# The second image's group-norm statistics in pieces of 512 pixels, and two residual chunks in the keys' room

## The chip, the cores and the metric

The kernel runs on one core of a Trainium2 chip. A core has five engines that run side by side, each through its own list of instructions in order: TensorE (PE, matrix products), VectorE (DVE), ScalarE (ACT), GpSimd (POOL) and SyncE (SP). Here SP only issues DMA transfers; ACT issues some as well, between its own work. The metric is the device time of the program in microseconds (us); a run's number is the median over the executions shown.

## The reference

Two residual layers over two images of 512 channels and 64 x 64 pixels, in float32:

```python
# --- layer 0 (conv_preact) ---
x = x + _L0_conv_ref(_gn(x), ...)      # deformable convolution, groups of 32 channels
# --- layer 1 (conv_preact) ---
x = x + _L1_conv_ref(_gn(x), ...)      # attention over the 4096 pixels, batch norm, relu
...
def _gn(v, G=32, eps=1e-5):
    B_, C_, H_, W_ = v.shape
    g = v.reshape(B_, G, C_ // G, H_, W_)
    m = jnp.mean(g, axis=(2, 3, 4), keepdims=True)
    s = jnp.var(g, axis=(2, 3, 4), keepdims=True)
    return ((g - m) / jnp.sqrt(s + eps)).reshape(v.shape)
```

Layer 0 normalizes its input by groups of 16 channels, projects it (`in_w`), and from a depthwise 3 x 3 convolution, a layer norm and a GELU it makes offsets and masks, with which the projection is sampled; `out_w` and the residual follow. Layer 1 normalizes again, makes keys, queries and values, applies softmax attention, and then a batch norm over both images, relu and the residual. The last residual is layer 0's result, so it is read once more at the very end.

## The kernel before

**Layer 0** works in 16 chunks of 512 pixels, eight per image. Each chunk passes through four stages, written as Python generators: `project` (normalize on ACT into `xn`, project on PE, store to `xt` in DRAM), `features` (the nine taps of the convolution: tap 1 on ACT at L790, eight on VectorE at L795 for each of four channel blocks; then the layer norm with two PE sums `p_mean`, L808, and the GELU, L832), `weights` (offsets and masks: PE `po`, L849, VectorE L854 to L897, then `at`, `awT` by PE transposes and ACT copies, L900 and L909) and `sample` (PE `pb` and ACT copies into `bt`, L942; PE `pa`, L956, with ACT copies into `dT`, L967; PE `py`, L976; the residual on VectorE, L981; result stored as `wx`). From L1135 on the order is written out by hand: `period` (L1005) calls single steps of these generators of different chunks, and each engine's list has the order in which these calls are made. In the names of `period`, `f` is a step of `features` of chunk i+2, `w` of `weights` of i+1, `m` of `sample` of i, `y` and `v` the ends of `sample` and `weights` of the chunks before, `p` of `project` of i+3 and `more` a step of the statistics. A period takes about 70 us.

**The statistics** of the input are made by `image_stats` (L704): `bn_stats` on VectorE over pieces, one `bn_aggr` for each channel block, then `group_norm_steps` (L604), a chain between PE, VectorE and ACT. Image 0 is in SBUF as a whole at the start. For image 1 pieces of 256 pixels are loaded by SP into three rotating buffers `xraw`, three ahead, and each call of `more` runs one `bn_stats` and issues the load of a later piece. There are 64 pieces; a period calls `more` 13 times, five periods long. Before the sixth period `run(later)` finishes what is left: the aggregate and the group norm's chain. SP also issues, in its order, `raw` (input rows for `project`, L744), `patch` (what is sampled, L921, eight transfers a time), `res`, `xt` and `wx`.

The key and query weights `wkq` are used only in layer 1 (L1356). They have a buffer of their own and are loaded by SP before the first period (L1131).

**Layer 1** is a loop over the images, and for each over eight query chunks `qb` (L1380). For each, 16 pairs of key blocks `kp` and two further steps accumulate in six PSUM banks (`acc`, L1417); `produce` (L1257) makes scores from `kq` (the keys of an image, 16 KB a partition) two steps ahead. A last product `p7` (L1455) follows; three of its operands `v7` are loaded only while it runs. After the last chunk the residual of image 1 is needed: once `acc` is done, the pools `w1in` (which holds `kq`), `w1v` and `w1vv` are closed (L1441), a pool `rp` of eight buffers of 1 MB is laid over their room, and ACT issues eight loads (L1445). Then come the batch norm's constants (L1518 to L1525) and the final loop: relu on ACT (L1530), the residual's sum on VectorE (L1534), the store by SP (L1535), first image 1, then image 0, whose chunks and residuals are fetched by SP (L1512) into buffers that become free.

Every transfer issued by SP or ACT takes one of eight semaphores in turn, over both engines, and its issuer waits until the transfer eight earlier has landed; this comes from the layer that builds the program.

Of the kernel before, what the change touches and what calls it, by code (L numbers as in the profile page):

```python
# [9 lines left out]
F32 = mybir.dt.float32  # L10
# [7 lines left out]
P = 128  # L18
NB = 2
C = 512  # L20
KB = C // P
H = W = 64
S = H * W
# [7 lines left out]
CH = 512  # L31
NCH = S // CH
# [5 lines left out]
DQ = 64  # L38
# [532 lines left out]
def window_path(ctx: ExitStack, tc: tile.TileContext, t_in: dict, out: bass.AP, far: bass.AP, sums: bass.AP):  # L571
# [26 lines left out]
    norm0 = []  # L598


    wkq = const.tile([P, KB, 3, DQ], F32, name="wkq")
    al = const.tile([P, 1], F32, name="al2")

    def group_norm_steps(mv, k, small, psum, result):  # L604
# [30 lines left out]
    with ExitStack() as l0:  # L635
# [68 lines left out]
        def image_stats(n):  # L704

            mv = sm.tile([P, KB, 2], F32, name="gn_mv")
            size = CH if n == 0 else CH // 2
            pieces, ahead = deque((kb, h) for kb in range(KB) for h in range(S // size)), deque()
            for kb in range(KB):
                st = sm.tile([P, 16, 6], F32, name="gn_st")  # L710
                for h in range(S // size):
                    if n == 0:
                        t = img[kb][:, h * size : (h + 1) * size]
                    else:
                        while len(ahead) < 3 and pieces:
                            k2, h2 = pieces.popleft()
                            ahead.append(io.tile([P, size], F32, name="xraw", bufs=3))
                            nc.sync.dma_start(ahead[-1], x_v[n, :, k2, h2 * size : (h2 + 1) * size])
                        t = ahead.popleft()
                    nc.vector.bn_stats(st[:, h, :], t)  # L720
                    yield
                nc.vector.bn_aggr(mv[:, kb, :], st[:, : S // size].rearrange("p a b -> p (a b)"))
            yield
            result = []
            yield from group_norm_steps(mv, KB, sm, ps, result)
            sc, bi = result
            gn[n] = [sm.tile([P, KB], F32, name=f"gn_{k}{n}") for k in ("scale", "bias")]
            nc.vector.tensor_copy(gn[n][0], sc)
            nc.vector.tensor_copy(gn[n][1], bi)
# [275 lines left out]
        def period(y, v, m, w, f, g, p, more):  # L1005

            p()  # L1010
            y()
            v(4)
            f(4)
            y()
            for taps in (9, 7, 6, 6):
                m(2)
                w()
                more()
                f(taps)
                w()  # L1020
                more()
            w()
            m()
            w()
            m()
            f()
            y()
            f()
            m()
            p()  # L1030
            w(2)
            y(2)
            w()
            m()
            p()
            f()
            w(2)
            p()
            y(2)
            f()  # L1040
            y()
            m()
            p()
            more()
            for k, steps in enumerate((1, 2, 2, 2)):
                p()
                w(steps)
                if k == 0:
                    f()
                p()  # L1050
                more()
                if k < 3:
                    m()
                if k == 0:
                    f()
                if k == 2:
                    g()
            w()
# [68 lines left out]
        run(features(1), project(2), output_bias())  # L1127
        fetch(0, 0)
        fetch(0, 1)
        for k, name in enumerate(("wkT", "wqT", "wkT")):  # L1130
            nc.sync.dma_start(wkq[:, :, k, :], t_in[name].rearrange("(kb p) m -> p kb m", p=P))  # L1131
        for h in range(2):
            nc.sync.dma_start(al[h * DQ : (h + 1) * DQ, :], t_in["L1_conv_align_w"])
        later, y, f = image_stats(1), Chain(sample, NSEQ), Chain(features, 2)
        with tc.manual_schedule():  # L1135
            f()
            for i in range(NSEQ):
                if i == NCH - 3:
                    run(later)
                w, m, g = Chain(weights, i + 1), Chain(sample, i), Chain(features, i + 3)  # L1140
                if i + 2 >= NSEQ:
                    (next_to_last if i + 1 < NSEQ else last_period)(y, v, m, w)
                    y, v = m, w
                    continue
                period(y, v, m, w, f, g, Chain(project, i + 3), lambda: next(later, None))
                y, v, f = m, w, g
            y.rest()
# [5 lines left out]
    with ExitStack() as l1, tc.manual_schedule():  # L1153
# [8 lines left out]
        with ExitStack() as at, ExitStack() as inner:  # L1162
            aw = at.enter_context(tc.tile_pool(name="w1w", bufs=1))
            wk = at.enter_context(tc.tile_pool(name="w1work", bufs=2))
            iw = inner.enter_context(tc.tile_pool(name="w1in", bufs=1, side="right", reuse_waits="tile"))
            vw = inner.enter_context(tc.tile_pool(name="w1v", bufs=3, side="right"))
            vv = inner.enter_context(tc.tile_pool(name="w1vv", bufs=3, side="right"))
            ps = at.enter_context(tc.tile_pool(name="w1ps", bufs=1, space=PSUM))
# [170 lines left out]
            for n in range(NB):  # L1339
# [40 lines left out]
                for qb in range(NCH):  # L1380
                    acc = {}
                    for kp in range(NPAIR + 2):
                        if kp + 2 < NPAIR:
                            produce(qb, kp + 2)
                        if kp == NPAIR - 1:

                            pr = ps.tile([P, 2, CH], F32, tag="st", name="pr")[:, 0, :]
                            nc.tensor.matmul(pr, ones, tots.pop(qb), start=True, stop=True)
                            nc.vector.tensor_mul(xq, xq, pr.unsqueeze(1).to_broadcast([P, KB, CH]))
                            x4 = xq.rearrange("p (h r) (j q) -> p h r j q", h=2, j=2)  # L1390
                            tx = wk.tile([P, 2, 4, HQ], F32, tag="tx", name="tx", bufs=1)
                            nc.vector.tensor_sub(tx[:, :, 3, :], x4[:, 1, :, 1, :], x4[:, 0, :, 1, :])
                            nc.vector.tensor_add(tx[:, :, 0, :], tx[:, :, 3, :], x4[:, 0, :, 0, :])
                            nc.vector.tensor_sub(tx[:, :, 2, :], tx[:, :, 0, :], x4[:, 1, :, 0, :])
                            nc.vector.tensor_sub(tx[:, :, 1, :], x4[:, 0, :, 1, :], x4[:, 0, :, 0, :])
                            rin = wk.tile([P, CH], F32, name="rin", bufs=1)
                            nc.vector.reciprocal(rin, pr)
                        nxt = qb * NPAIR + min(kp, NPAIR) + 2
                        if kp < NPAIR and nxt < NCH * NPAIR:
                            ready.append(load_values(n, nxt % NPAIR))  # L1400
                        if kp == 2:
                            xq = wk.tile([P, KB, CH], F32, tag="x", name="xq", bufs=1)
                            nc.sync.dma_start(xq, x1_d[n][qb])
                        if 3 <= kp < NPAIR:
                            v7s[kp - 3] = load_seventh(n, kp - 3)
                        if kp < NPAIR:
                            v = ready.pop(0)
                            e, tt, _ = made[qb, kp]
                            ops = operands(lambda k: e[:, k, :], tt)
                        else:  # L1410
                            v = w7[:, kp - NPAIR]
                            ops = operands(lambda k: x4[:, k // 2, kp - NPAIR, k % 2, :], tx[:, kp - NPAIR])
                        for j in (3, 4, 5, 2, 1, 0) if kp == 0 else (0, 1, 4, 2, 3, 5) if kp == NPAIR else range(6):
                            if kp == 0:
                                acc[j] = bank(j, f"acc{j}")
                            for cb in range(2):
                                nc.tensor.matmul(  # L1417
                                    acc[j][:, cb * HQ : (cb + 1) * HQ], v[:, j, cb * P : (cb + 1) * P], ops[j],
                                    start=(kp + cb == 0), stop=(kp + cb == NPAIR + 2),
                                )  # L1420
                        next(rest, None)
                        if kp == 6:
                            normalize(xq, sc, bi)
                        if kp == 8 and qb + 1 < NCH:
                            queries(qb + 1)
# [13 lines left out]
                    if n + 1 == NB and qb + 1 == NCH:  # L1439

                        inner.close()  # L1441
                        rp = l1.enter_context(tc.tile_pool(name="w1res", bufs=NCH, side="right", reuse_waits="tile"))
                        for ch in range(NCH):
                            res.append(rp.tile([P, KB, CH], F32, tag="xr", name="xr"))
                            nc.scalar.dma_start(res[ch], x1_d[n][ch])  # L1445

# [139 lines left out]
```

## Time and profile before

| | us |
|---|---|
| median of 3 runs (lowest, highest) | 3688.65 (3687.94, 3691.09) |
| the profiled execution | 3685.08 |
| its span, first to last instruction | 3683.3 |
| PE busy | 3410.6 (93%) |
| VectorE busy | 2344.1 (64%) |
| ACT busy | 1307.4 (35%) |
| `conv` on VectorE (L795), 512 instructions | 399.7 |
| `bn_stats` of image 1, 256 pixels, 64 instructions | 25.8, with 8.3 of waits for their loads |
| `bn_stats` of 512 pixels, one | 0.68 |
| `acc` on PE (L1417), 6144 instructions | 1516.5 |

The profile is of one execution. A line of a group gives the line of the program, engine and operation, the tiles, how often, the busy time, the mean of one, and the engine's idle time ahead of these instructions with what ended most of it. A line of a timeline gives start and length in us, then the same, with the idle time ahead in brackets. A line of the table of stretches gives from:to and length, then for each engine its busy time and how many instructions it started, the granted clock of TensorE (1.00 is full), the busy share of the DMA engines and GB/s. Layer 0 ends at about 1255 us.

### The profile page before, as it was taken

What the parts mean: (1) busy time and instruction counts of PE and PEld (TensorE: products, weight loads), DVE (VectorE), ACT (ScalarE), POOL (GpSimd) and SP (SyncE); (2) the same over time, 40 slices, a digit from 0 to 9 for tenths busy, and PEclk for the clock granted to TensorE, in tenths of its full rate; (3) what the DMA queues carried; (4) which work ended last, traced back from release to release, by engine and by line L of the source; (5) the groups of instructions that cost most, each with busy time, mean ns of one, the idle gap of its engine ahead of it and who ended that gap; (6) DMA issues with size and microseconds to landing.
All of it is one profiled execution on the core that took longest, in us unless ns stands there. A gap on an engine that the chain in (4) does not pass through costs nothing.

```text
span 3683.3 us, 39025 instructions
## 1 busy us (share of the span) xinstructions
PE 3410.6 (93%) x15155; PEld 2430.9 (66%) x15155; DVE 2344.1 (64%) x3581; ACT 1307.4 (35%) x1694; POOL 291.5 (8%) x190
## 2 busy tenths in 40 slices
PE   4589998999998999999999999999999999999990
PEld 1355555555555677777777777787777777777770
DVE  5798989999998575554554554467455455545544
ACT  2476777787886421111111111121111111111114
POOL 2112111211211020000000000021000000000000
PEclk9789999999999999999999999999999999999995
DMA  7233442342331444334334433434333343343349
GB/s 245 63 99 112 134 142 83 112 136 85 119 118 66 159 166 174 124 113 160 123 108 145 137 127 115 153 146 187 130 127 116 114 139 112 104 147 122 112 159 395
DMA packets 179653, 499.93 MB, mean 136 GB/s; under 512 B 22112, under 2 KB 63840, under 8 KB 169984
## 3 DMA queue, kind: packets, MB, share of 16 engines
q1 hardware_dynamic: 175680, 471.11, 38.0%
q10 hardware_dynamic: 3744, 26.22, 1.9%
q8 instruction: 121, 1.98, 0.2%
q14 instruction: 76, 0.62, 0.0%
q0 software_dynamic: 32, 0.00, 0.0%
HBM read 405.96 MB, written 91.29 MB: 135 GB/s over the span
## 4 chain that ended last, share of the span: by engine, by line
PE 76%; DVE 14%; DMA 4%; ACT 2%; SPq 1%; issue 1%; POOL 1%; ACTq 0%; DVEq 0%; POOLq 0%
PE acc L1417 42%; DVE conv L795 8%; PE pS L1262 7%; PE p L1455 7%; PE py L976 5%; PE pa L956 4%; PE pv L1302 4%; PE pq L765 4%; PE pk L1356 1%; PE p_mean L808 1%; DMA patch<-xt 1%; DMA out<-ct 1%; DVE o L854 1%; DMA in_w<-in_L_conv_in_w 1%; DVE rstd L827 1%
## 5 line engine op out<-in xcount | busy, mean ns | idle before, releaser
L1417 PE MATMUL acc<-e,v 128*128 128x256 f32 x3072 | 768.3, 386 | 0.0
L1266 ACT ACTIVATE e<-pS 128x1024 f32<-128x1024 f32 x256 | 262.4, 1025 | 1385.9 <-PE pS L1262 1317.5
L1417 PE MATMUL acc<-tt,v 128*128 128x256 f32 x3072 | 748.2, 380 | 0.3
L1417 PEld LDWEIGHTS acc<-e,v 128*128 128x128 f32 x3072 | 566.5, 190 | 233.2 <-issue 165.4
L1417 PEld LDWEIGHTS acc<-tt,v 128*128 128x128 f32 x3072 | 582.4, 190 | 91.0 <-issue 10.6
L1269 DVE TENSOR_TENSOR t<-e 128x256 f32<-128x256 f32 x256 | 108.9, 425 | 761.2 <-ACT e L1266 761.2
L795 DVE SCALAR_TENSOR_TENSOR conv<-xn,L_conv_dw_w_sb,conv 128x504 f32<-128x504 f32 (+1 forms) x512 | 399.7, 795 | 48.4 <-ACT conv L790 36.4
L1279 DVE TENSOR_TENSOR tot<-tot,e 128x512 f32<-128x512 f32 x480 | 330.1, 688 | 8.3
L956 PEld LDWEIGHTS pa<-bt,patch 96*128 96x128 f32 x2048 | 253.0, 198 | 62.8 <-issue 35.1
L1262 PE MATMUL pS<-q,kq 64*128 64x512 f32 x1024 | 289.0, 641 | 0.0
L956 PE MATMUL pa<-bt,patch 96*128 96x128 f32 x2048 | 256.9, 283 | 12.5 <-ACT dT L967 5.8
L942 ACT COPY bt<-pb 96x1024 f32<-96x1024 f32 x124 | 234.7, 2006 | 56.5 <-PE pb L937 56.5
L765 PE MATMUL pq<-in_w,xn 128*128 128x512 f32 x512 | 235.8, 604 | 4.1 <-ACT xn L755 4.1
L976 PE MATMUL py<-dT,L_conv_out_w_sb 128*128 128x512 f32 x512 | 239.0, 612 | 0.0
L1455 PE MATMUL p<-t,v 128*128 128x256 f32 x1024 | 231.6, 382 | 1.9 <-DMA v<-wv 1.9
L1455 PEld LDWEIGHTS p<-t,v 128*128 128x128 f32 x1024 | 192.1, 190 | 48.8 <-issue 21.2
L967 ACT COPY dT<-pa 32x256 f32<-32x256 f32 x496 | 179.9, 363 | 73.5 <-PE pa L956 64.8
L849 PE MATMUL po<-om_w_pg,feat 128*128 128x432 f32 x512 | 200.9, 537 | 0.0
L976 PEld LDWEIGHTS py<-dT,L_conv_out_w_sb 128*128 128x128 f32 x512 | 99.5, 198 | 121.8 <-issue 117.3
L765 PEld LDWEIGHTS pq<-in_w,xn 128*128 128x128 f32 x512 | 93.9, 194 | 108.8 <-issue 93.2
L849 PEld LDWEIGHTS po<-om_w_pg,feat 128*128 128x128 f32 x512 | 92.7, 189 | 89.4 <-issue 88.1
L1262 PEld LDWEIGHTS pS<-q,kq 64*128 64x128 f32 x1024 | 77.1, 184 | 84.9 <-issue 84.9
(204 smaller groups left out, 3721.5 us busy)
## 6 DMA issues: line engine op xcount, KB each, us to landing
v<-wv SPq DMA_DIRECT2D x252, 768.0 KB
patch<-xt SPq DMA_DIRECT2D x256, 192.0 KB
v<-wv SPq DMA_DIRECT2D x256, 128.0 KB
wv<-v SPq DMA_DIRECT2D x32, 896.0 KB
xt<-xj SPq DMA_DIRECT2D x128, 128.0 KB
res<-in_x SPq DMA_DIRECT2D x64, 256.0 KB
wx<-res SPq DMA_DIRECT2D x64, 256.0 KB
xq<-wx SPq DMA_DIRECT2D x16, 1024.0 KB
```

The source lines that it names most:

```text
L765: nc.tensor.matmul(pq, xn[:, kb, 1 + 2 * t : 3 + 2 * t, :].rearrange("p r c -> p (r c)"), in_w[:, kb, :], start=(kb == 0), stop=(kb == KB ...
L795: nc.vector.scalar_tensor_tensor(dst, src, wt, dst, ALU.mult, ALU.add)
L849: nc.tensor.matmul(po[:, : 3 * GP], f[:, kb, t * P : (t + 1) * P], om_w[:, kb].rearrange("p a k g -> p (a k g)"), start=(kb == 0), stop=(k ...
L942: copy(bt[:SN].rearrange("s g q d -> s d (g q)")[:, d0 : d0 + 4, :], pb[:SN])
L956: nc.tensor.matmul(pa[:, p], xp[:SN, p, cb * P : (cb + 1) * P], bt[:SN, 4 * cb : 4 * cb + 4, PX * s + p, :], start=True, stop=True,)
L967: copy(dst, src)
L976: nc.tensor.matmul(py, out_w[:, kb, cb * P : (cb + 1) * P], dT[:, kb, :], start=(kb == 0), stop=(kb == KB - 1))
L1262: nc.tensor.matmul(pS[:, h, :], kq[r, 2 * (kp // 4) + h, c0 : c0 + P], qs[qb][r, :], start=True, stop=True)
L1266: nc.scalar.activation(e.rearrange("p a q -> p (a q)"), pS.rearrange("p h q -> p (h q)"), AF.Exp)
L1279: nc.vector.tensor_add(tots[qb], tots[qb], e2[:, h, :])
L1417: nc.tensor.matmul(acc[j][:, cb * HQ : (cb + 1) * HQ], v[:, j, cb * P : (cb + 1) * P], ops[j], start=(kp + cb == 0), stop=(kp + cb == NPAI ...
L1455: nc.tensor.matmul(p7[:, cb * HQ : (cb + 1) * HQ], v7[:, cb * P : (cb + 1) * P], t3, start=(k + cb == 0), stop=(k + cb == NPAIR + 2),)
```

## The change

There are two parts.

1. The statistics of image 1 use 32 pieces of 512 pixels, loaded by ACT's queue. Two of the three buffers are the halves of a new tile `early` (4 KB a partition); the third is one `xraw`. `wkq` becomes a view of `early`, so its loads move behind the last `bn_stats`, after `run(later)`. A period calls `more` six times, at other places: ahead of the first four taps, behind these, behind the first and the second `weights` piece among the taps, once ahead of the layer norm's `rstd`, and once in the last loop. 30 pieces fall to five periods, and `run(later)` does the last two as well.
2. The pool `w1in` stays open to the end. Two of the eight residual chunks of image 1 go into `kq`'s room, with loads that ACT issues at the step after the last scores were made (`kp` = 14 of the last chunk); `rp` has six buffers and is loaded as before.

```diff
--- before.py
+++ after.py
@@ -598,7 +598,9 @@
     norm0 = []
 
 
-    wkq = const.tile([P, KB, 3, DQ], F32, name="wkq")
+
+    early = const.tile([P, 2, CH], F32, name="early")
+    wkq = early.rearrange("p a q -> p (a q)")[:, : KB * 3 * DQ].rearrange("p (kb k d) -> p kb k d", kb=KB, k=3)
     al = const.tile([P, 1], F32, name="al2")
 
     def group_norm_steps(mv, k, small, psum, result):
@@ -704,22 +706,23 @@
         def image_stats(n):
 
             mv = sm.tile([P, KB, 2], F32, name="gn_mv")
-            size = CH if n == 0 else CH // 2
-            pieces, ahead = deque((kb, h) for kb in range(KB) for h in range(S // size)), deque()
+            room = [early[:, 0], early[:, 1], io.tile([P, CH], F32, name="xraw")] if n else []
+            pieces, ahead = deque((kb, h) for kb in range(KB) for h in range(NCH)), deque()
             for kb in range(KB):
-                st = sm.tile([P, 16, 6], F32, name="gn_st")
-                for h in range(S // size):
+                st = sm.tile([P, NCH, 6], F32, name="gn_st")
+                for h in range(NCH):
                     if n == 0:
-                        t = img[kb][:, h * size : (h + 1) * size]
+                        t = img[kb][:, h * CH : (h + 1) * CH]
                     else:
+
                         while len(ahead) < 3 and pieces:
                             k2, h2 = pieces.popleft()
-                            ahead.append(io.tile([P, size], F32, name="xraw", bufs=3))
-                            nc.sync.dma_start(ahead[-1], x_v[n, :, k2, h2 * size : (h2 + 1) * size])
+                            ahead.append(room[len(pieces) % 3])
+                            nc.scalar.dma_start(ahead[-1], x_v[n, :, k2, h2 * CH : (h2 + 1) * CH])
                         t = ahead.popleft()
                     nc.vector.bn_stats(st[:, h, :], t)
                     yield
-                nc.vector.bn_aggr(mv[:, kb, :], st[:, : S // size].rearrange("p a b -> p (a b)"))
+                nc.vector.bn_aggr(mv[:, kb, :], st.rearrange("p a b -> p (a b)"))
             yield
             result = []
             yield from group_norm_steps(mv, KB, sm, ps, result)
@@ -1010,15 +1013,17 @@
             p()
             y()
             v(4)
+            more()
             f(4)
+            more()
             y()
             for taps in (9, 7, 6, 6):
                 m(2)
                 w()
-                more()
                 f(taps)
                 w()
-                more()
+                if taps in (7, 9):
+                    more()
             w()
             m()
             w()
@@ -1037,18 +1042,19 @@
             w(2)
             p()
             y(2)
+            more()
             f()
             y()
             m()
             p()
-            more()
             for k, steps in enumerate((1, 2, 2, 2)):
                 p()
                 w(steps)
                 if k == 0:
                     f()
                 p()
-                more()
+                if k == 2:
+                    more()
                 if k < 3:
                     m()
                 if k == 0:
@@ -1127,16 +1133,16 @@
         run(features(1), project(2), output_bias())
         fetch(0, 0)
         fetch(0, 1)
-        for k, name in enumerate(("wkT", "wqT", "wkT")):
-            nc.sync.dma_start(wkq[:, :, k, :], t_in[name].rearrange("(kb p) m -> p kb m", p=P))
-        for h in range(2):
-            nc.sync.dma_start(al[h * DQ : (h + 1) * DQ, :], t_in["L1_conv_align_w"])
         later, y, f = image_stats(1), Chain(sample, NSEQ), Chain(features, 2)
         with tc.manual_schedule():
             f()
             for i in range(NSEQ):
                 if i == NCH - 3:
                     run(later)
+                    for k, name in enumerate(("wkT", "wqT", "wkT")):
+                        nc.sync.dma_start(wkq[:, :, k, :], t_in[name].rearrange("(kb p) m -> p kb m", p=P))
+                    for h in range(2):
+                        nc.sync.dma_start(al[h * DQ : (h + 1) * DQ, :], t_in["L1_conv_align_w"])
                 w, m, g = Chain(weights, i + 1), Chain(sample, i), Chain(features, i + 3)
                 if i + 2 >= NSEQ:
                     (next_to_last if i + 1 < NSEQ else last_period)(y, v, m, w)
@@ -1162,7 +1168,7 @@
         with ExitStack() as at, ExitStack() as inner:
             aw = at.enter_context(tc.tile_pool(name="w1w", bufs=1))
             wk = at.enter_context(tc.tile_pool(name="w1work", bufs=2))
-            iw = inner.enter_context(tc.tile_pool(name="w1in", bufs=1, side="right", reuse_waits="tile"))
+            iw = l1.enter_context(tc.tile_pool(name="w1in", bufs=1, side="right", reuse_waits="tile"))
             vw = inner.enter_context(tc.tile_pool(name="w1v", bufs=3, side="right"))
             vv = inner.enter_context(tc.tile_pool(name="w1vv", bufs=3, side="right"))
             ps = at.enter_context(tc.tile_pool(name="w1ps", bufs=1, space=PSUM))
@@ -1419,6 +1425,11 @@
                                     start=(kp + cb == 0), stop=(kp + cb == NPAIR + 2),
                                 )
                         next(rest, None)
+                        if n + 1 == NB and qb + 1 == NCH and kp + 2 == NPAIR:
+
+                            for ch in range(2):
+                                res.append(kq[:, KB * ch : KB * (ch + 1), :])
+                                nc.scalar.dma_start(res[ch], x1_d[n][ch])
                         if kp == 6:
                             normalize(xq, sc, bi)
                         if kp == 8 and qb + 1 < NCH:
@@ -1439,8 +1450,8 @@
                     if n + 1 == NB and qb + 1 == NCH:
 
                         inner.close()
-                        rp = l1.enter_context(tc.tile_pool(name="w1res", bufs=NCH, side="right", reuse_waits="tile"))
-                        for ch in range(NCH):
+                        rp = l1.enter_context(tc.tile_pool(name="w1res", bufs=NCH - 2, side="right", reuse_waits="tile"))
+                        for ch in range(2, NCH):
                             res.append(rp.tile([P, KB, CH], F32, tag="xr", name="xr"))
                             nc.scalar.dma_start(res[ch], x1_d[n][ch])
```

## The prediction

> **What bounds the kernel now.** I read the page's chain of waits first: which engine holds the end, stage by stage.
>
> ```profile
> PE acc L1417 42%; DVE conv L795 8%; PE pS L1262 7%; PE p L1455 7%; PE py L976 5%; PE pa L956 4%; PE pv L1302 4%; PE pq L765 4%; PE pk L1356 1%; PE p_mean L808 1%; DMA patch<-xt 1%; DMA out<-ct 1%; DVE o L854 1%; DMA in_w<-in_L_conv_in_w 1%; DVE rstd L827 1%
> ```
>
> Layer 1 (from about 1255 us) is TensorE's, and the change touches it only at its very end. In layer 0 VectorE (conv L795) and TensorE share the path. So I next cut layer 0 at the starts of `my` (L884), which comes once a period, and read the busy-time table of these stretches:
>
> ```profile
> core 0: us, PE busy (x) PEld busy (x) DVE busy (x) ACT busy (x) POOL busy (x), PEclk, DMA share, GB/s
> 283.13:359.72 76.59, 67.54 (x312) 39.48 (x311) 67.24 (x86) 54.32 (x74) 12.99 (x10) 0.93 0.41 122
> 359.72:433.97 74.25, 66.79 (x308) 39.14 (x307) 66.53 (x85) 53.35 (x72) 12.98 (x10) 0.95 0.40 126
> 433.97:508.22 74.25, 67.20 (x312) 39.44 (x311) 67.05 (x87) 55.02 (x76) 12.97 (x10) 0.98 0.39 125
> 508.22:583.49 75.27, 66.46 (x310) 39.26 (x309) 65.27 (x85) 53.68 (x71) 12.97 (x11) 0.93 0.34 104
> 583.49:654.20 70.71, 67.47 (x318) 39.75 (x317) 62.68 (x72) 55.80 (x77) 12.98 (x11) 1.00 0.35 108
> 654.20:721.91 67.71, 64.50 (x310) 38.31 (x309) 62.68 (x73) 53.86 (x73) 13.00 (x10) 1.00 0.37 113
> ```
>
> A plain period takes 67.7 us at full clock. Those with statistics of the second image take 74 to 77, at a lower clock; the one before these (210.31 to 283.13) takes 72.8. Over six periods the excess is 444 - 6 x 67.7 = 38 us. The timelines of PE and VectorE say what it is made of:
>
> ```profile
> 273.86 2.07 PE L808 MATMUL p_mean<-tot,ones_c 128*128 128x512 f32 x2 [5.75 <-POOL tot L803]
> 275.73 5.75 PE L976 MATMUL py<-dT,L_conv_out_w_sb 128*128 128x512 f32 x8
> ...
> 712.63 1.12 PE L808 MATMUL p_mean<-tot,ones_c 128*128 128x512 f32 x2 [1.23 <-POOL tot L803]
> 713.59 3.60 PE L976 MATMUL py<-dT,L_conv_out_w_sb 128*128 128x512 f32 x8
> ```
>
> ```profile
> 242.90 0.69 DVE L982 BATCH_NORM_STATS2 stats<-res 128x6 f32<-128x512 f32 x1
> 243.51 0.41 DVE L720 BATCH_NORM_STATS2 gn_st<-xraw 128x6 f32<-128x256 f32 x1
> 243.84 6.85 DVE L795 SCALAR_TENSOR_TENSOR conv<-xn,L_conv_dw_w_sb,conv 128x504 f32<-128x504 f32 x9
> ...
> 253.02 0.43 DVE L720 BATCH_NORM_STATS2 gn_st<-xraw 128x6 f32<-128x256 f32 x1 [1.48 <-DMA xraw<-in_x]
> ```
>
> The period's cycle is: VectorE's taps, then POOL's `tot`, then p_mean on PE, then PE's py/pa/pq without a gap, then ScalarE's conv (L790), then the next taps. Whatever stands between the first and the last tap delays p_mean. With statistics there PE idles 5 to 7 us before p_mean instead of 1.23, and the next ten matmuls run slow: 2.07 + 5.75 us against 1.12 + 3.60, 3.1 us more. A step from one start to the next is 0.33 us for 256 pixels and 0.61 for 512.
>
> The end, by the same table: DMA stands still, then is full to the last.
>
> ```profile
> 3560.00:3570.00 10.00, 10.00 (x46) 8.42 (x45) 6.38 (x6) 0.00 (x0) 0.00 (x0) 1.00 0.00 0
> 3570.00:3575.00 5.00, 5.00 (x25) 4.40 (x24) 1.85 (x1) 0.26 (x1) 0.00 (x0) 1.00 0.00 0
> 3580.00:3585.00 5.00, 5.00 (x25) 4.41 (x24) 2.07 (x1) 0.00 (x0) 0.00 (x0) 1.00 1.01 424
> 3640.00:3650.00 10.00, 0.00 (x0) 0.00 (x0) 4.99 (x3) 6.52 (x10) 0.00 (x0) 0.50 1.02 414
> ```
>
> **What the Trainium skill says.** "TensorE: Matmul & The Clock Gate", Part 1: PE falls to half clock after a window of about 3.4 us without enough work, and the windows run free. The trace agrees: gaps of 4.35 to 7.1 us before p_mean were followed by half clock, eight gaps of 1.2 us (periods from 645 us on) were not; a gap of 2.5 us (1294.4) wasn't, one of 1.76 (1230.6) was. "DMA: Bandwidth & Descriptors", Issuing engines are not separate DMA queues: transfers from SP and ACT share the same DMA engines, so ACT's queue adds no bandwidth. Its section Queues, rings and completion order: the engines take turns between the queues, so a load issued by ACT needn't wait behind all that SP has queued. The trace of before has no such load in layer 0, so there it can't be checked.
>
> **The change, part by part.**
>
> *Statistics on the path.* Before, a period has 13 pieces of 256; seven lie between first and last tap: 7 x 0.335 = 2.35 us, and one waits 1.5 to 2.7 us there for its load, which SP issued behind eight patches. After, six pieces of 512. One stands before the first tap and one before `res` (L981), where VectorE waits in a plain period anyway (1.82 us for ScalarE's conv, 1.42 for py): nothing. Two stand among the taps: 1.22 us. Two lie in the TensorE half. With the first they fill the 1.82 us (3 x 0.61), and one of them puts ScalarE's gelu back 0.6 us, of which its 0.73 us gap, less a DMA issue in it, hides most: I add 0.25. So a period is 67.7 + 1.22 + 0.25 = 69.2 us, if the clock holds.
>
> *Load issues on ACT.* 32 of some 0.37 us (as the 64 from SP took). Where they are put ScalarE waits in the plain period: 1.21, 0.38 and 1.15 us around the bt copies, 0.83 and 0.73 around dT. Hidden; uncovered they would be 6 x 0.37 = 2.2 us a period. Each load also waits for its room's bn_stats (one call back, long done) and, as the program shares eight DMA semaphores in turn among SP and ACT, for the transfer eight earlier to land: the fourth and the sixth patch, xt, raw. By the timeline the patches are issued in 0.7 us steps from the first tap on; the sixth should land by 9 us, when ACT comes there. Behind ACT stand the bt copies, and pa and p_mean behind these, with 2.4 us to spare.
>
> *The start.* Before, SP loaded the first pieces at 139.8 us. After, ACT issues them behind the awT copies, which end at 175.7, while VectorE has its first bn_stats ahead of the first tap (170.73). With 2.4 us to land, as a load in the next period took (issued 233.41, used 235.86), plus 0.3 us for the double size, the taps begin at 179.0. After the lighter pieces of that period `my` comes at 217.4 instead of 210.3: 7.1 us lost, once.
>
> *Group norm and key weights.* Two pieces and the aggregate now stand before the group norm's chain: 1.2 us, in the 4.7 us that VectorE waits there for ScalarE's `gn_var`. The five key-weight loads leave SP's queue at 78 us and come back behind these bn_stats, ahead of the raw loads, which have some 40 us: nothing for either; before 170 us I bound it by -1 and +1 us.
>
> *Sum of layer 0:* 217.4 + 4 x 69.2 + (75.27 - 1.4) = 568.1 for the sixth `my`, against 583.5: -15.4 us. (The 1.4 is the rstd wait in that period, due to the cold clock before it.) The clock is what isn't known: PE's gap before p_mean becomes 1.23 + 1.22 = 2.4 us. Bounds: no half clock (0), or about 2.2 us in each of four periods (+9). I take +4: **-11.4 us.**
>
> *The end.* Two of eight residual chunks (2.1 MB) move to the stretch at 3553 us, behind the last exp, where DMA is soon idle. They leave a queue that is full at 415 GB/s: 2.1 / 0.415 = 5.05 us. p7 then waits less for its v7 loads (2.7 us), so the first output is ready 2.6 us earlier. Small gaps in the stream cost 1 to 2 us, since ScalarE gives a chunk each 2.8 us and DMA needs 2.5. Bounds -5.5 and -2.5, **taken -4 us.**
>
> Total -15.4: 3685.1 (the profiled execution: its span 3683.3 and 1.8 around it) gives 3669.7. The median shown is 3.55 above that execution, so 3673.2.
>
> **The rivals.**
> 1. *The clock stays cold.* 2.4 us of gap are still enough in each period: -15.4 + 9 - 4 = -10.4, 3678. For it: the gap of 1.76 us that was followed by half clock. Against: the one of 2.5 that wasn't.
> 2. *The pieces wait for their own loads.* From 398 to 404 us DMA moves 300 to 404 GB/s (three raw loads). If two pieces a period wait 1.8 us each over four periods, 14.4 us come back: -1, 3687, no change.
> 3. *ScalarE is held at the queue (the slower side).* If the patch, xt or raw transfer that an ACT load waits for lands late, ACT stands still ahead of the bt copies and all of layer 0 behind it. Up to 2.4 us a period is hidden; at 8 us in each of five periods it is 5 x 5.6 = 28 us, the total +13: 3701. It decides from 2.4 + 15.4/5 = 5.5 us a period. Against: patches were landing by about 11.6 us after the first tap at the latest.
>
> That the change doesn't do what it says can be left out: 32 pieces, 30 in the periods' calls and two in the closing run, stand in the program.
>
> **How the numbers follow.** Forecast 52% (3666 to 3682 by its bounds), rival 1 20%, rival 2 15%, rival 3 13%. This kernel's measurement tells 0.2% (7.4 us) from no change: the forecast and rival 1 lie below 3681, so faster 72%, same 15%, slower 13%. The range reaches from 3665 (no cold clock, end at its best: -15.4 - 5.5, and 3 more) to 3688, which leaves out rival 3.
>
> **What would show it.** Right: `my` near 217 in the first period, then periods near 69 us; p_mean's gap 2 to 3 us; no wait of bn_stats for DMA but the first, 8 us or more after the last work; L942 waiting for PE alone; 200 GB/s or more between 3553 and 3562. Wrong: bn_stats rows with waits for DMA in each period, idle ScalarE ahead of L942 ended by a DMA, a clock below 1.00 in each period, or an unchanged distance from the last acc matmul to the end.

## The result, and the profile after

The changed kernel takes 3677.86 us (median of 10 runs, 3675.72 to 3680.51), the kernel before beside it 3687.7 (10 runs, 3683.93 to 3691.09): ratio 0.9975, 95% interval 0.9965 to 0.9985. That is 9.8 us faster, where the forecast said 15.4.

I read the profile after in the same order as the one before. First the table of stretches, cut at the starts of `my` (now L887), for the six periods from the first on and a plain one:

```profile
218.37:288.90 70.53, 61.63 (x280) 37.16 (x281) 64.75 (x74) 54.26 (x74) 14.61 (x11) 0.93 0.39 120
288.90:359.92 71.02, 66.28 (x309) 38.78 (x308) 66.33 (x79) 53.57 (x73) 13.05 (x10) 0.98 0.41 130
359.92:431.18 71.26, 66.19 (x310) 38.93 (x309) 66.68 (x80) 53.84 (x73) 13.03 (x10) 0.98 0.40 129
431.18:502.05 70.87, 66.42 (x314) 38.98 (x313) 66.70 (x80) 54.86 (x74) 13.04 (x10) 1.00 0.40 129
502.05:575.90 73.85, 65.07 (x307) 38.61 (x306) 66.36 (x85) 52.88 (x70) 13.03 (x11) 0.93 0.37 115
575.90:646.63 70.73, 67.46 (x317) 39.77 (x317) 62.73 (x73) 55.77 (x77) 13.03 (x11) 1.00 0.34 108
646.63:714.36 67.73, 64.50 (x310) 38.32 (x309) 62.75 (x73) 53.83 (x73) 13.08 (x10) 1.00 0.38 113
```

The first `my` stands at 218.37 (forecast 217.4). The four statistics periods take 70.5 to 71.3 us where before they took 72.8 to 76.6; the forecast was 69.2, plus 1 for the clock. The group norm's period takes 73.85 (forecast 73.87). The sixth `my` is 7.6 us ahead of before, or 9.1 when both are counted from their chunk 0's `my`, which came 1.5 us later in this execution (forecast 11.4).

The start, in the timelines of VectorE and ScalarE:

```profile
173.03 0.16 DVE L1127 TENSOR_TENSOR L_conv_out_b_sb<-L_conv_out_b_sb,p_bias 128x4 f32<-128x4 f32 x1 [8.71 <-PE p_bias L1123]
179.06 0.69 DVE L723 BATCH_NORM_STATS2 gn_st<-early 128x6 f32<-128x512 f32 x1 [5.87 <-DMA early<-in_x]
```

```profile
175.24 1.07 ACT L912 COPY awT<-p_tr 128x512 f32<-128x512 f32 x2
176.08 0.34 ACTq L721 DMA_DIRECT2D early<-in_x  x1
```

The first piece comes at 179.06 and, one step of 0.61 later, the taps at 179.67. The forecast had the taps at 179.0. The load took 3.0 us from issue (176.08) to use; 2.7 was forecast.

Next, TensorE's timeline around `p_mean` in the third and fourth period:

```profile
421.87 1.38 PE L811 MATMUL p_mean<-tot,ones_c 128*128 128x512 f32 x2 [3.10 <-POOL tot L806]
423.04 5.08 PE L979 MATMUL py<-dT,L_conv_out_w_sb 128*128 128x512 f32 x8
...
492.74 1.12 PE L811 MATMUL p_mean<-tot,ones_c 128*128 128x512 f32 x2 [2.50 <-POOL tot L806]
493.70 3.60 PE L979 MATMUL py<-dT,L_conv_out_w_sb 128*128 128x512 f32 x8
```

The gap is 2.5 to 3.1 us, near the forecast's 2.4, instead of 5 to 7. Behind the gap of 3.10 the next matmuls are slow, behind the one of 2.50 they aren't. And VectorE among the taps of the third period:

```profile
400.90 0.60 DVE L857 TENSOR_TENSOR o<-po,om_b_pg 128x432 f32<-128x432 f32 x1
402.07 0.69 DVE L723 BATCH_NORM_STATS2 gn_st<-xraw 128x6 f32<-128x512 f32 x1 [0.57 <-DMA xraw<-in_x]
402.68 1.51 DVE L798 SCALAR_TENSOR_TENSOR conv<-xn,L_conv_dw_w_sb,conv 128x504 f32<-128x504 f32 x2
```

One piece still waits for its load in the second, third and fourth period: 0.50, 0.57 and 0.17 us. Its load was issued at 395.82, 6.2 us before it was read.

The end, in the table of stretches:

```profile
3550.00:3555.00 5.00, 5.00 (x25) 4.40 (x24) 2.52 (x6) 0.00 (x0) 0.00 (x0) 1.00 1.00 386
3555.00:3560.00 5.00, 5.00 (x23) 4.03 (x22) 0.08 (x1) 0.00 (x0) 0.00 (x0) 1.00 0.48 202
...
3575.00:3600.00 25.00, 16.78 (x77) 13.78 (x76) 11.27 (x24) 3.40 (x5) 0.50 (x2) 0.87 1.02 420
3600.00:3605.00 5.00, 0.00 (x0) 0.00 (x0) 2.82 (x4) 5.00 (x8) 0.00 (x0) 0.50 0.80 329
3605.00:3610.00 5.00, 0.00 (x0) 0.00 (x0) 4.18 (x2) 5.00 (x8) 0.00 (x0) 0.50 0.85 327
3610.00:3615.00 5.00, 0.00 (x0) 0.00 (x0) 3.94 (x3) 5.00 (x8) 0.00 (x0) 0.50 0.99 331
3615.00:3620.00 5.00, 0.00 (x0) 0.00 (x0) 3.95 (x3) 5.00 (x9) 0.00 (x0) 0.50 1.03 356
3620.00:3640.00 20.00, 0.00 (x0) 0.00 (x0) 16.31 (x8) 19.10 (x28) 0.00 (x0) 0.50 1.02 417
```

The kernel before, at the same place behind its first output:

```profile
3605.00:3610.00 5.00, 0.00 (x0) 0.00 (x0) 2.56 (x4) 5.00 (x8) 0.00 (x0) 0.50 1.02 421
3610.00:3615.00 5.00, 0.00 (x0) 0.00 (x0) 4.47 (x2) 5.00 (x8) 0.00 (x0) 0.50 1.00 400
```

The two chunks do move in the idle stretch (386 GB/s from 3550 on). But from 3600 to 3620 us the transfers now run at 327 to 356 GB/s, where before they kept to 400 or more. At 415 that is (86 + 88 + 84 + 59) GB/s x 5 us = 1.6 MB not moved, 3.8 us of the 5.05 us that had left the queue. By the column of the busy share the DMA engines stood idle for about half of this, (0.20 + 0.15 + 0.01) x 5 us = 1.8 us; for the other 2 us they were busy, at a lower rate.

The stretches of every profiled execution (us), from the starts of `my` and the last `acc`. "Start" is from chunk 0's `my` to the first period's, "periods" from there to the sixth, "middle" from the last of the sixteen `my` to the end of `acc`, "end" from there to the end of the span:

| kernel | median (before beside it) | start | periods | middle | end |
|---|---|---|---|---|---|
| before | | 84.2 | 373.2 | 2400.2 | 104.3 |
| changed | 3677.86 (3687.7) | 90.7 | 357.5 | 2404.1 | 102.7 |
| part1_only | 3678.77 (3687.42) | 90.8 | 357.2 | 2402.6 | 103.9 |
| part2_only | 3684.08 (3687.42) | 83.7 | 374.2 | 2398.9 | 103.1 |
| primed | 3670.51 (3687.42) | 83.7 | 362.4 | 2400.6 | 102.8 |
| off_taps | 3716.26 (3687.42) | 91.6 | 398.9 | 2400.6 | 102.9 |
| off5 | 3660.42 (3689.35) | 84.4 | 345.4 | 2402.0 | 102.7 |
| warm | 3672.67 (3689.35) | 90.8 | 354.9 | 2401.7 | 102.3 |
| fin4 | 3674.71 (3689.35) | 90.7 | 357.7 | 2403.7 | 101.2 |
| sp_loads | 3677.10 (3689.35) | 84.0 | 368.5 | 2400.7 | 102.8 |
| act_queue | 3693.45 (3687.69) | 89.5 | 373.6 | 2402.4 | 104.3 |
| best | 3657.69 (3687.69) | 84.0 | 345.5 | 2405.1 | 100.6 |

The changed kernel's own row against before: start +6.5, periods -15.7, end -1.5, together -10.7. The middle scatters from 2398.9 to 2405.1 over these executions, though its query chunks take 129.75 us each, in both the kernel before and the changed one. The two differ there by 3.9 us, so two profiled executions can't be subtracted as wholes; the medians (-9.8) come close to the sum of the other three stretches.

### The profile page after: what moved, and what is told of

Same layout as the page of the kernel before. It is cut to its first block, busy times and chain, and to the rows that moved or that the text cites. A ratio compares the mean times of both kernels' runs of the same rounds, so it can differ in the third digit from the quotient of the medians.

```text
span 3678.2 us, 38948 instructions
## 1 busy us (share of the span) xinstructions
PE 3412.8 (93%) x15155; PEld 2432.7 (66%) x15155; DVE 2351.4 (64%) x3549; ACT 1306.7 (36%) x1694; POOL 292.7 (8%) x190
## 4 chain that ended last, share of the span: by engine, by line
PE 78%; DVE 13%; DMA 4%; ACT 2%; issue 1%; POOL 1%; SPq 1%; ACTq 0%; DVEq 0%; POOLq 0%
PE acc L1423 42%; DVE conv L798 9%; PE pS L1268 7%; PE p L1466 6%; PE py L979 5%; PE pq L768 5%; PE pa L959 5%; PE pv L1308 3%; PE pk L1362 1%; PE p_mean L811 1%; DVE o L857 1%; DMA v<-wv 1%; DMA in_w<-in_L_conv_in_w 1%; DMA xraw<-in_x 0%; DMA r<-wc 0%
```

## The experiments

**Each part alone.** part1_only takes the second part out of the changed kernel, part2_only puts it alone into the kernel before.

```diff
 (part1_only)
-            iw = l1.enter_context(tc.tile_pool(name="w1in", ...
+            iw = inner.enter_context(tc.tile_pool(name="w1in", ...
-                        if n + 1 == NB and qb + 1 == NCH and kp + 2 == NPAIR:
-                            for ch in range(2):
-...
-                        for ch in range(2, NCH):
+                        for ch in range(NCH):
```

> The changed kernel without its second part: all eight residual chunks are loaded after the last acc again. Theory (part 1 is worth what the starts of my show, -7.5 us, and part 2 only what the last stretch shows, -1.5): 3680 us, my as in the changed kernel (first period's at 218.4, the sixth at 576, 7.5 ahead of before), last acc to the end of the span 104.3 us as before. Rival (part 2 is worth the 4 us that the prediction gave it, and part 1 the rest): 3682, sixth my at 578 or later. If the half-clock stretches fall where chance puts them in an execution, the single periods may differ from the changed kernel's by 1.7 us each.

> The kernel before with the second part alone: two residual chunks in the keys' room. Theory (the moved loads leave a hole in the transfers before the first output, and only the end of p7 moves, by 1 us): 3686, last acc to the end of the span 102.8, less than 400 GB/s for some 15 us after p7. Rival (prediction's -4: the queue gets shorter by 5 us and stays full): 3683.7, last acc to end 100.3.

part1_only: ratio 0.9977 (0.997 to 0.9984), 3678.77 us. part2_only: 0.9994 (0.9985 to 1.0003). Part 1 is nearly the whole gain; in time alone part 2 can't be told from nothing. The trace shows more: from the last `acc` to the end it is 103.9 to 104.3 in the three kernels without part 2, and 102.3 to 103.1 in the seven that have it and no other change at the end, 1.4 us in the mean. That excludes the prediction's 4 us.

**The first loads early.** In `primed` the first three pieces are loaded by SP ahead of the first period.

```diff
+            if n:
+                for _ in range(3):
+                    load_piece(nc.sync)
+                yield
...
         later, y, f = image_stats(1), Chain(sample, NSEQ), Chain(features, 2)
+        next(later)
```

> The changed kernel with its first three pieces loaded by SP ahead of the first period instead of by ACT behind the awT copies. Theory (the 7 us at the start are the wait for the first load, nothing else): no wait of the first bn_stats, first tap near 172.5, first my at 211.5 instead of 218.4, the whole 3671. Rival (what is gained at the start is lost again in the first periods, since taps there wait for something else or the clock falls once more): first my no earlier than 216, 3676 or more.

Ratio 0.9953 (0.9937 to 0.997), 3670.51 us, 7.3 less than the changed kernel. The start is 83.7 us again. VectorE's timeline has no wait for a load there:

```profile
170.44 1.52 DVE L805 SCALAR_TENSOR_TENSOR conv<-xn,L_conv_dw_w_sb,conv 128x504 f32<-128x504 f32 x2
171.88 0.69 DVE L730 BATCH_NORM_STATS2 gn_st<-early 128x6 f32<-128x512 f32 x1
```

The first `my` came at 207.56, earlier than expected, since this execution's chunk 0 was also some 4 us ahead; the stretch is the measure. The periods gave back 4.8 us: their waits for `xraw` were 1.21, 0.60 and 0.71, and the group norm's period took 76.4. So the start's loss is shown, and that the loads in the periods are tight as well.

**No piece among the taps, first attempt.** `off_taps` puts the two pieces from among the taps ahead of the first tap and ahead of `res`.

```diff
             v(4)
             more()
+            more()
             f(4)
             more()
+            more()
             y()
...
-                if taps in (7, 9):
-                    more()
```

> The changed kernel with the two pieces among the taps moved: two now stand ahead of the first tap and two ahead of res. Theory (a period's excess is the two pieces among the taps, 1.5 us, and the half clock that the longer gap before p_mean brings, 1.7): gap before p_mean 1.3 us, clock 1.00, second to fourth period 68.0 to 68.4 us instead of 70.5 to 71.3, the whole 3666. Rival (loads: a piece close behind another has 4 us at most to land, in the stretch where patches are loaded): bn_stats waits 1 to 2 us for DMA twice a period, periods 70 or more, 3675 to 3679.

The rival, and far worse than its numbers: ratio 1.0079 (1.0063 to 1.0096), 3716.26 us. ScalarE's and VectorE's timelines show why:

```profile
412.19 0.33 ACTq L721 DMA_DIRECT2D xraw<-in_x  x1
412.28 0.62 ACT L912 COPY awT<-p_tr 128x512 f32<-128x512 f32 x1
413.90 1.68 ACTq L721 DMA_DIRECT2D early<-in_x  x2
419.18 0.34 ACTq L721 DMA_DIRECT2D xraw<-in_x  x1
419.55 3.68 ACT L945 COPY bt<-pb 96x1024 f32<-96x1024 f32 x2 [6.65 <-DMA raw<-in_x]
```

```profile
418.45 0.69 DVE L723 BATCH_NORM_STATS2 gn_st<-xraw 128x6 f32<-128x512 f32 x1 [10.77 <-DMA xraw<-in_x]
419.80 0.69 DVE L723 BATCH_NORM_STATS2 gn_st<-early 128x6 f32<-128x512 f32 x1 [0.66 <-DMA early<-in_x]
```

A load is issued where `more` is called, and in ScalarE's list that place lies behind `at` and the `awT` copies, at 412. VectorE is at its place at 407.7 and waits 10.8 us; the load takes 6.3. ScalarE's load at 419.18 waits for that very piece, as its room must be read first, and behind it stand the `bt` copies, idle for 6.65 us (the releaser that the line names, `raw`, is only the last that landed). The loads before it were held as well. The chain of waits, in order of time, shows by what:

```profile
407.07 6.76 DMA patch<-xt
413.83 0.03 ACTq L721
413.86 0.04 issue
413.90 5.88 DMA early<-in_x
```

The load at 413.90 had to wait until a patch had landed. So this is the prediction's third rival at work: ScalarE is held at its queue, first by the transfers that it named (the trace has a second such wait, to 415.15; up to there 2.3 of the 6.65 us have passed), and then, for longer, by a room that had not been read, which the prediction called "long done".

**No piece among the taps, with the loads in time.** `off5` separates the load from the piece. Six pieces are done ahead of the first period; a period has five.

```diff
+        for _ in range(3):
+            load_piece(nc.sync)
         with tc.manual_schedule():
+            for _ in range(6):
+                next(later)
+                load_piece(nc.sync)
...
             more()
+            more()
             f(4)
             more()
             y()
...
-                if taps in (7, 9):
-                    more()
+                if k < 3:
+                    load_piece()
...
+                if k == 1:
+                    load_piece()
                 if k == 2:
                     more()
+                    load_piece()
```

> The changed kernel with no piece among the taps, in a way that gives each load time: six pieces are done ahead of the first period, with loads by SP; a period has five (two ahead of the first tap, one ahead of res, the two in the TensorE half as before), and each load is issued by ACT where its room has long been read and at least 5 us ahead of its use. Theory (a period's excess is the pieces among the taps, their waits for loads, and the half clock that follows): gap before p_mean 1.2 to 1.3 us, clock 1.00 in the second to fourth period, these 67.9 to 68.4 us, first my near 206, sixth near 553, the whole 3655. Rival (loads are late wherever they are issued beside the patches, as in off_taps): bn_stats waits 2 us or more for DMA in each period, periods of 70 us or more, 3665 or more.

Ratio 0.9921 (0.9908 to 0.9935), 3660.42 us. The table of stretches, from the first period's `my` on:

```profile
211.33:279.61 68.28, 60.94 (x284) 36.44 (x285) 63.77 (x72) 55.05 (x75) 14.60 (x11) 0.95 0.37 120
279.61:347.38 67.77, 64.52 (x310) 38.34 (x309) 65.84 (x79) 53.91 (x73) 13.05 (x10) 1.00 0.42 133
347.38:415.10 67.72, 64.47 (x310) 38.30 (x309) 65.43 (x77) 53.83 (x73) 13.04 (x10) 1.00 0.42 132
415.10:482.90 67.80, 64.48 (x310) 38.34 (x309) 65.89 (x78) 53.78 (x73) 13.05 (x10) 1.00 0.41 131
```

The periods are plain ones, though VectorE is busy for 65.8 us of 67.8 instead of 62.7: at their places five pieces cost nothing. That holds for the piece ahead of `rstd` too, for which I had charged 0.25. The first `my` was 5 us later than expected: the early pieces waited 7.7 us for their loads in chunk 0's time, chunk 0 was 3 us later than in primed (in the executions without early pieces it lies anywhere from 123.8 to 127.7), and the start took 84.4. In the periods no piece waited for a load.

**The clock alone.** `warm` fills part of the gap before `p_mean` in the changed kernel with matmuls that read weights and whose result is overwritten.

```diff
-            def mean_over_c(tot):
+            def mean_over_c(tot, extra=0):
                 p = ps.tile([P, CH], F32, tag="mm", name="p_mean")
+                for _ in range(extra):
+                    nc.tensor.matmul(p, ones, in_w[:, 0, :], start=True, stop=True)
...
-            mu = mean_over_c(tot)
+            mu = mean_over_c(tot, 2 if 3 <= i <= 6 else 0)
```

> The changed kernel with two more matmuls of p_mean's size just ahead of p_mean for chunks 3 to 6; they read weights and their result is overwritten. They fill 1.7 us of the gap. Theory (half clock behind p_mean costs 1.5 to 1.7 us a period): no half clock there, the second p_mean 11.4 us behind the first, periods of 69.2 to 69.8, sixth my near 571, 3673. Rival (the periods are long because of the pieces ahead of rstd and among the taps, and the clock's share would be hidden): clock 1.00 but periods still 70.5 or more, 3678.

Ratio 0.9958 (0.9943 to 0.9973), 3672.67 us. TensorE's timeline in the first period:

```profile
272.95 1.88 PE L812 MATMUL p_mean<-in_w,ones_c 128*128 128x512 f32 x4
275.90 1.13 PE L813 MATMUL p_mean<-tot,ones_c 128*128 128x512 f32 x2 [1.07 <-POOL tot L806]
276.87 3.60 PE L981 MATMUL py<-dT,L_conv_out_w_sb 128*128 128x512 f32 x8
...
287.31 1.02 PE L813 MATMUL p_mean<-sq,ones_c 128*128 128x512 f32 x2
```

The second `p_mean` is 11.4 us behind the first in all four periods; in the changed kernel it was 12.91, 13.10, 13.10 and 11.40. The second and fourth period took 69.7, the third 71.05, since its piece now waited 2.04 us for its load. The waits for `xraw` grew from 1.24 to 3.15 us in sum: a part of what the clock gives back is taken by the loads.

**The hole at the end.** `fin4` allows a fourth pair of chunks of image 0 to be fetched ahead of the final loop.

```diff
-        fin = l1.enter_context(tc.tile_pool(name="w1fin", bufs=3, ...
+        fin = l1.enter_context(tc.tile_pool(name="w1fin", bufs=4, ...
...
-        ready = [fetch(ch) for ch in range(3)]
+        ready = [fetch(ch) for ch in range(4)]
```

> The changed kernel with four instead of three pairs of chunks of image 0 fetched ahead of the final loop (2 MB more in flight before the first output). Theory (the 2 MB that were moved left a hole of 3.8 us before and behind the first output, since no transfer was allowed to start): the hole is filled, 400 GB/s or more throughout, last acc to the end of the span 99 to 100 us instead of 102.8, 3674. Rival (the end is the first output and sixteen steps of ScalarE and stores behind it, and loads don't matter): last acc to end stays at 102 to 103, 3678.

Ratio 0.9961 (0.9946 to 0.9976), 3674.71 us; last `acc` to end 101.2. The table of stretches around the first output:

```profile
3597.50:3602.50 5.00, 0.00 (x0) 0.00 (x0) 2.56 (x4) 5.00 (x8) 0.00 (x0) 0.50 1.01 424
3602.50:3607.50 5.00, 0.00 (x0) 0.00 (x0) 4.47 (x2) 5.00 (x8) 0.00 (x0) 0.50 1.01 323
3607.50:3612.50 5.00, 0.00 (x0) 0.00 (x0) 3.95 (x3) 5.00 (x8) 0.00 (x0) 0.50 1.01 381
```

By these lines 0.6 MB are missing at 415 GB/s instead of 1.6, and the end is 1.5 us shorter. The share is 1.01 in all three: no engine stands idle any more, and what came back is about the 1.8 us of idle time that the changed kernel had. So it is shown that the idle part of the hole came from transfers that weren't allowed to start. The size expected (3 to 4) is not reached; what is still missing is rate while the engines are busy, and its cause wasn't tried.

**Queue or places?** `sp_loads` is the changed kernel with its loads on SP's queue, `act_queue` the kernel before with its loads on ACT's; in each one word changes (`nc.scalar` to `nc.sync`, and the reverse).

> The changed kernel with its pieces loaded by SP instead of ACT, at the same places of the program. Theory (the issuing queue matters, since SP's list has the patches and raw loads with their waits ahead of a piece): bn_stats waits 1 us or more for DMA in most periods, 2 to 4 us a period longer, 3686 to 3694. Rival (all loads share the DMA engines, so the issuer is of no account): waits and periods as in the changed kernel, 3676 to 3680.

> The kernel before with its 64 pieces of 256 pixels loaded by ACT instead of SP, places unchanged. Theory (the queue is worth most of the gain in the periods and the places among the taps the rest): waits of bn_stats for DMA 0.5 us or less a period, but seven pieces among the taps still, periods of 71.5 to 73.5 instead of 72.8 to 76.6, first my 5 to 7 us later, about 3685. Rival (thirteen issues a period hold ScalarE ahead of bt): ScalarE's idle time ahead of L942 ends with a DMA, periods of 75 or more, 3695 or more.

sp_loads: ratio 0.9971 (0.9959 to 0.9983), 3677.1 us; the total is the rival's, but the stretches aren't. Its four statistics periods take 71.5 to 74.1 with waits for `xraw` of 1.4 to 3.0 each and the group norm's takes 76.9, 11 us in sum more than the changed kernel's, and its start is 6.7 shorter, because SP issues the first loads early. Most of the one cancels the other; the 4 us that remain don't show in the medians (3677.1 against 3677.86), and the middle of this execution is 3.4 us shorter. act_queue: ratio 1.0013 (1.0007 to 1.002), slower, against my theory. Its periods take as long as before (373.6), with 7.9 us of waits of `bn_stats` for DMA in them against 8.3, and the start loses 5.3, with 5.0 of wait for the first load. ScalarE's group of `bt` copies between 218 and 502 us:

```profile
L942 ACT COPY bt<-pb 96x1024 f32<-96x1024 f32 x32 | 60.1, 1987 | 19.4 <-PE pb L937 12.0 <-DVE gn_st L720 4.4 <-DVE conv L795 2.6
```

Before, this group was idle for 12.7 us, all for PE; here ScalarE also waits for `gn_st`, whose room its load needs. So in the periods ACT's queue gains nothing at the old places and 11 us at the new ones (368.5 to 357.5), and the new places and sizes gain 4.7 us (373.2 to 368.5) with SP's queue, 16 (373.6 to 357.5) with ACT's. That it is the distance between the pieces that decides is argued, not tried alone.

**Together.** `best` is off5 with fin4 and with five extra matmuls in the group norm's period.

```diff
-            mu = mean_over_c(tot)
+            mu = mean_over_c(tot, 5 if i == 7 else 0)
```

> What paid in the runs before, together: no piece among the taps and loads in time (off5), four pairs of chunks fetched ahead of the final loop (fin4), and five extra matmuls of p_mean's size ahead of p_mean in the group norm's period (chunk 7), whose gap of 5 to 7 us was followed by half clock in every run. Theory: periods as in off5, the group norm's period and the next 3 us shorter in sum than off5's 73.9 and 69.2 (the second back at 67.7), last acc to end 101.2, off5's 3660.4 less 1.5 for the cold clock and less 3 at most for the end: 3656 to 3658. Rival (the group norm's period is held by VectorE's chain alone and the loads' order at the end differs from execution to execution): 3660.

Ratio 0.992 (0.9907 to 0.9934), 3657.69 us: 30 us less than before and 20 less than the changed kernel. The gap ahead of `p_mean` in the group norm's period is 0.78, and the period behind it takes 67.68 instead of 69.15; the group norm's own period stays at 73.84, so half clock isn't what holds it. That VectorE's chain does, as the rival says, was not tried. By time alone the two additions can't be told from off5.

## Why the prediction was right or wrong

- *The start:* right. +7.1 forecast, +6.5 measured, and the taps at 179.67 for 179.0, in an execution whose chunk 0 was 1.5 us later.
- *Pieces among the taps:* the place was right, the term too small. 1.22 a period, 4.9 in four, was forecast. From the first tap on, the four periods were 1.58, 1.79, 1.85 and 1.46 us longer than a plain one, 6.7. Of the 1.8 us between, 1.24 are waits for loads. The step that failed is "no wait but the first": I took 2.4 us from a load of half the size, in a stretch where DMA moved 214 GB/s, plus 0.3; beside patches and `raw`, where it moved 333 GB/s (395.8 to 402.1 us), a load took 6.2. The other 0.6 us are not accounted for. So the second rival had a grain of truth, 1.2 us of its 14.4.
- *The clock:* taken at +4, bounds 0 and +9, with 0.25 a period for the piece ahead of `rstd`: 5 in sum. Measured: the first tap came 1.23, 1.51, 1.69 and 1.69 us later behind `my` than in a plain period, 6.1. The last three are the second `p_mean`'s delays in the period before (1.51, 1.70, 1.70). Here the piece ahead of `rstd` cost nothing, as VectorE waits there anyway. warm shows that the clock's share is real.
- *The group norm's period:* right, 73.85 for 73.87.
- *The end:* wrong in size, and the largest miss: -4 forecast, -1.4 measured. The step that failed: two chunks "leave a queue that is full at 415 GB/s", with "small gaps" for 1 to 2 us. The queue was full because the loads just lasted until the first output; only three pairs may be fetched ahead of it, so taking 2.1 MB from the stretch before costs 3.8 us of transfers there, 1.8 of them with idle engines (fin4 shows the cause of these) and 2.0 at a lower rate (cause open). What is left behind the first output is the same sixteen stores and ten loads. The first output itself came 1.0 us earlier behind the last `acc`, not 2.6, and only 0.2 earlier than in part1_only: SP, free earlier, issued its first `r<-wc` while `v7` was still landing. That this load delayed `v7` is argued from the order in the trace, not tried.
- *Sum:* +7.1 - 18.5 - 4 against +6.5 - 15.7 - 1.5. Direction and the mechanism of the first part were right, that of the second in part; the size was more than half too large. The first rival's 3678 fits the measured time, but not as a cause: it had half clock in all four periods (it was three) and kept the -4 at the end.
- *ScalarE held at the queue* did not happen in the changed kernel beyond its first period (5.7 us of `bt` waiting for `gn_st`, inside the start's loss). From the second period on ScalarE was idle ahead of its first `bt` copy for 1.69 us at most, against 1.21 in a plain period. off_taps shows that it needs only other places.

## What to carry to other kernels

Price a load by how long one takes in the stretch where it will run, and place its issue on the engine's list by that time, not by where its data are used: with the same pieces, places and issue times decided between 3716 and 3660 us. Before counting bytes taken out of a full queue as time, look at what the queue would move next and whether it is allowed to start. And compare two profiles stretch by stretch, over several executions: here a stretch that the change doesn't touch scatters by 6 us.

## What the hardware showed that I had not expected

- Half clock comes in pieces of one length, on one grid. By the clock record of the changed kernel's trace it lasted 3.41 us behind `p_mean` in each of the first three statistics periods (from 279.25, 350.93 and 422.61 us), 6.83 us twice before that (from 207.57, in a gap of 7.14, and from 221.22), and 10.24 us in the group norm's period (from 562.56, in a gap of 6.67). These are one, two and three times 3.413 us, and the starts lie multiples of 3.413 us apart; so do all changes of the clock in each of the twelve traces, to 0.001 us. This fits the free windows of about 3.4 us of the Trainium skill, "TensorE: Matmul & The Clock Gate", Part 1. The second `p_mean` stands 11.40 us behind the first without half clock; 13.10 behind most shorter gaps, and up to 14.5 behind the long gaps of before.
- So whether a gap is followed by half clock isn't decided by its length alone. Gaps of 2.50, 2.60 and 2.61 us were followed by 11.40, gaps of 1.95, 2.52 and 2.64 by 13.10, in the same place of the same loop. The changed kernel's third and fourth period, cut at this grid (busy time of TensorE alone, and its clock):

```profile
419.20:422.61 3.41, 0.74 (x2) 1.00 0.01 2
422.61:426.02 3.41, 3.41 (x5) 0.50 0.00 0
490.88:494.29 3.41, 1.55 (x4) 1.00 0.00 0
494.29:497.70 3.41, 3.41 (x14) 1.00 0.00 0
```

The gap of 3.10 us left TensorE idle for 2.67 us of one window, and the next was at half clock. The gap of 2.50 us fell into two windows, with 1.86 us idle in the one shown, and the next stayed at full clock. The same cut sorts all twelve such gaps of the changed kernel, part1_only and fin4: 1.95 to 2.80 us idle in one window in the nine that were followed by half clock, at most 1.86, 1.72 and 1.49 us in the three that weren't. A limit can't be read from this: in primed 1.56 us in one window was followed by half clock. From the second period on a gap of 1.2 us never was.

- The same 256 KB load took 3.0 us at the start (DMA moved 202 GB/s) and 6.2 to 6.3 beside patches and `raw` (333 GB/s in the changed kernel's third period), from issue to use.
